# Last batch's down product joins x through the identity, fillers counted one by one, new leads

## The chip, the cores and the metric

The kernel runs on one core of one Trainium2 chip. The core's engines work in parallel, each in the order of its own instruction list: TensorE (PE in the profile; its weight loads are the row PEld), VectorE (DVE), ScalarE (ACT), GpSimd (POOL) and SyncE (SP), which issues the transfers between memory and on-chip storage. [...] The metric is the device time of one execution in microseconds, lower is better.

## The reference

There are 8 batches of 1024 rows with 128 features, all in f32. Cut to what matters, and with the weights that scale and shift left out:

```python
mod = (silu(c) @ wmod).reshape(8, 6, 1, 128)          # six vectors a batch: sa ca ga sb cb gb
h = layernorm(x) * (1 + ca) + sa
y = h
for i in range(6):                                    # six layers of linear attention and an MLP
    xn = layernorm(y)
    q, k, v = heads(xn @ wq[i]), heads(xn @ wk[i]), heads(xn @ wv[i])     # 8 heads of 16
    context = softmax(k, over rows).T @ v
    y = (softmax(q, over features) @ context) @ wo[i] + bo[i] + y
    y = leaky(layernorm(y) @ w1[i]) @ w2[i] + y       # 128 -> 512 -> 128
x = x + ga * y
h = layernorm(x) * (1 + cb) + sb
g = silu(fp4(h) @ fp4(w_gate).T) * (fp4(h) @ fp4(w_up).T)                 # 128 -> 352
x = x + gb * (fp4(g) @ fp4(w_down).T)                 # 352 -> 128
```

`fp4` takes each run of 16 values along the last axis, divides by its largest magnitude over 6, rounds to the FP4 grid and multiplies back. The last line is where the first part of the change sits: the down product is added to `x`.

## The kernel before

A batch is a tile of 128 partitions by 8 chunks of 128 features, worked in two halves of 512 columns. Four batches are in flight at a time, each in its own set of buffers (a lane), so batch 4 takes the place of batch 0 and so on. A batch has eight stages: the first norm and modulation (0), six layers (1 to 6) and the FP4 feed-forward part (7).

Nothing is run when the loops are walked. Every piece of work is added to a plan as a step with its engine, its planned duration, what it reads and what it writes (`add`), and `order` then writes the program out by hand. At each turn it takes, over all engines, the step that can start earliest; among equals it takes the one with the longest chain behind it plus a *lead*. `LEAD` holds one lead per batch and stage, and `TURNS` changes leads at planned times, given as a time and a list of batch, stage and lead. A change of ScalarE's function table is planned at 1.3. The order so found is fixed on each engine by explicit dependences, so a step whose operands are late holds back everything behind it on its engine.

Fillers are part of that order. When the step chosen for TensorE starts later than the engine is free, by more than `GAP` (0.35), `order` puts 128 by 128 products of the identity with itself into the gap, while a PSUM bank is free and until `BRINK` (0.1) before its end. In the first 11.5 planned us (`COLD`) a TensorE step counts double, and a filler too. Whether fillers count double is settled once per gap: one that begins before 11.5 has all its fillers at double length, and half the threshold. A filler appears as `warm<-ident` on line 1361.

The lines that the prediction speaks of, in the order of a batch. `layernorm` takes statistics on VectorE (L641, L647), `rstd` on ScalarE (L661 and L666, a logarithm and an exponential), the small steps L671 to L687 on VectorE, and applies it half on VectorE (L693) and half on ScalarE (L700). The result (`xh_a` ahead of the attention, `xh_m` ahead of the MLP, `h` ahead of the FP4 part) is transposed on TensorE (L719) and copied out by ScalarE with the norm's weights (`xT`, L929). A layer then has the key product (L949), its largest value `nmax` on VectorE (L956, joined at L963), the exponential `kT` on ScalarE (L972), the query product (L996) with `qmax` (L1005), the context (L1059 to L1100), the output product (L1126) added to `x` on VectorE (L1111), the MLP's w1 product (L1172), its leaky activation on ScalarE (L1181) and the w2 product (L1189). While the first layers run, `prepare_attn` folds the bias rows of all six layers (`mb_bc`, L611, and `wv_sb`, L618, after small products at L591 and L602).

In the FP4 part, `fp4` quantises `h` and later the gated product `g`: a maximum per run (L747), its scale (L754) and reciprocal (L759), the quotient `fv` (L763) on VectorE, the magnitude `fmag` (L773) on ScalarE, two rounding steps (L777, L784) on VectorE and the product with the scale (L792) on GpSimd, or on VectorE for the very last piece. Gate and up products are L1233, silu is L1241 on ScalarE, the product of the two L1249 on VectorE. Silu needs another function table than the norm's logarithm and the exponentials, so table loads stand ahead of the first silu and ahead of the first exponential after it (L1241, L1372).

`down` then takes a piece of `g`: three transposes per chunk (L1289), two copies `gT` on ScalarE (L1302), three products per chunk into one bank (L1313), and the sum onto `x` on VectorE (L1322). A batch has four pieces of two chunks; the last batch has six pieces, chunks 0–1, 2–3, 4, 5, 6 and 7. SyncE sends `x` out (L1265): halves, or for the last batch quarters, when their chunks are done. A product of f32 operands is two records in the trace.

Of the kernel before, what the change touches and what calls it, by code (L numbers as in the profile page):

```python
# [11 lines left out]
ALU = mybir.AluOpType  # L12
AX = mybir.AxisListType

P = 128
# [68 lines left out]
class Plan:  # L84
# [58 lines left out]
    def order(self, leads, turns, warm):  # L143
# [17 lines left out]
        while todo:  # L161
# [22 lines left out]
            cold = 2 if e == "PE" and free[e] < self.COLD else 1  # L184
            gap = e == "PE" and t - free[e] > self.GAP / cold
            while gap and min(bank_free) <= free[e]:
                to = free[e] + cold * mm(P)
                if to > t - self.BRINK:
                    break
                w, bank = Step(), bank_free.index(min(bank_free))  # L190
                w.fn, w.func = lambda bank=bank: warm(bank), None
                free[e] = bank_free[bank] = to
                out.append(w)
# [42 lines left out]
def mm(n):  # L236

    return 0.0115 + n * 1.654e-3
# [11 lines left out]
def kernel(  # L250
# [41 lines left out]
        [2405, 3996, 461, 247, -1202, -1296, -1300, -3196],  # L292
        [1413, 1593, 3441, 1928, -2207, 1189, 1781, -248],
        [366, -108, -1676, -2703, -3835, 1594, -2630, -2514],
        [-241, 558, -1413, 208, -413, 228, -5405, -156],
        [694, -3633, -2192, -2384, -870, -487, -1194, -1272],
        [-3687, 2479, 1403, 3083, -1193, -6, -811, -1034],
        [725, 1777, 204, -1637, -400, -327, -320, -670],
        [3404, 589, 1158, 1867, -7, -962, -419, -2719],
# [3 lines left out]
        (3, [(1, 0, -62)]),  # L303
        (27, [(3, 0, -535)]),
        (36, [(2, 1, -485)]),
        (39, [(3, 1, -531)]),
        (45, [(0, 2, 1516), (2, 1, -553)]),
        (48, [(2, 1, -544)]),
        (57, [(1, 1, 1518), (1, 2, 2846), (1, 3, 649)]),
        (75, [(1, 1, 1516)]),  # L310
        (90, [(1, 1, 773)]),
        (105, [(0, 3, 2919), (0, 4, 1470), (0, 5, 1376), (0, 7, -524)]),
        (120, [(0, 3, 2762), (2, 1, -721)]),
        (150, [(1, 2, -201)]),
        (165, [(2, 1, 797)]),
        (180, [(1, 2, 1215)]),
        (210, [(2, 2, 832)]),
        (225, [(3, 1, 914), (3, 6, -4315)]),
        (240, [(0, 5, 828)]),
        (255, [(0, 5, 2639), (0, 6, 2635)]),  # L320
        (270, [(2, 3, 156)]),
        (285, [(0, 7, 811), (1, 3, 64)]),
        (300, [(4, 0, -33)]),
        (315, [(2, 2, 1013), (4, 0, 939)]),
        (330, [(3, 2, 544)]),
        (345, [(0, 7, 348), (2, 3, -400)]),
        (360, [(0, 7, 811), (2, 3, 1746), (2, 4, -2375)]),
        (405, [(1, 4, -3784), (4, 1, -3690)]),
        (420, [(1, 4, -3786)]),
        (435, [(2, 4, -3941)]),  # L330
        (450, [(1, 4, -2313)]),
        (465, [(4, 1, -4514)]),
        (480, [(1, 5, 1477)]),
        (495, [(3, 5, 1525)]),
        (525, [(1, 5, 1515), (2, 5, 1254)]),
        (555, [(1, 7, 1337)]),
        (570, [(2, 5, 1311)]),
        (600, [(1, 7, 1342)]),
        (615, [(1, 7, 1337), (3, 6, -3519), (5, 2, 2464)]),
        (630, [(3, 7, 1425)]),  # L340
        (675, [(5, 1, 2181)]),
        (690, [(4, 1, -2521)]),
        (705, [(2, 7, -2804), (4, 2, -2786), (4, 3, -4487), (4, 7, -1958)]),
        (735, [(5, 2, 3162)]),
        (780, [(6, 1, 323)]),
        (795, [(2, 7, -2027)]),
        (810, [(3, 7, 2088), (5, 3, 1769)]),
        (825, [(4, 3, -2043)]),
        (840, [(5, 4, -2386), (7, 1, 210), (7, 2, 779)]),
        (870, [(4, 3, -2494)]),  # L350
        (885, [(7, 1, 493)]),
        (915, [(6, 2, 913)]),
        (930, [(4, 3, -1826), (4, 4, -1241)]),
        (945, [(5, 4, -2139), (5, 6, -1878)]),
        (975, [(6, 3, -2917)]),
        (1005, [(7, 4, -2167)]),
        (1020, [(5, 5, -1207)]),
        (1035, [(5, 5, -1166)]),
        (1065, [(7, 4, -1977)]),
        (1140, [(4, 6, -2161), (5, 6, -1912)]),  # L360
        (1155, [(4, 6, -1857)]),
        (1170, [(4, 7, -1928)]),
        (1245, [(5, 7, -1905)]),
        (1260, [(6, 7, -139)]),
        (1275, [(6, 6, -1635)]),
        (1305, [(5, 7, -1974), (7, 7, 205)]),
        (1320, [(6, 7, -143), (7, 6, -143)]),
        (1335, [(6, 7, 201)]),
        (1350, [(6, 7, 206), (7, 7, 207)]),
    ]  # L370
    LATE = 140.0
    NQ = 4
# [829 lines left out]
    def ffn(x, mod, b, ln):  # L1202
# [51 lines left out]
        for i, c0, cn in PIECES[b == B - 1]:  # L1254
            down(gs[c0 // G], c0 % G, cn, c0, wdb, x, f"{b}_{c0}", i % 2, DVE_LAST and b == B - 1 and c0 + cn == C)
# [15 lines left out]
    def down(g, g0, G, c0, wdb, x, name, i, last):  # L1271
# [36 lines left out]

        def dmm():
            for c in range(G):  # L1310
                for m, (k, kk) in enumerate(KS):
# [3 lines left out]
                        wdb.ap()[:kk, m, :], start=(m == 0), stop=(m == NK - 1),  # L1315
                    )

        add("PE", G * NK * mm(D), dmm, r=[gT, wdb], w=[td])

        def onto():  # L1320
# [100 lines left out]
```

## Time and profile before

| | before |
|---|---|
| median of 4 runs | 1400.73 us (1400.33 to 1401.67) |
| the profiled execution | 1401.4 us, of which 1399.7 are the span from first to last instruction |
| mean granted TensorE clock | 0.999 of full speed |
| busy: PE, DVE, ACT, POOL | 1387.3, 1136.0, 967.0, 250.1 us |
| fillers (L1361) | 142 records, 20.7 us |
| table loads on ScalarE | 21, mean 1283 ns |
| x added to the down product (L1322) | 30 of 128x256 and 4 of 128x128, from 350.1 to 1396.8 us |

In the profile a line names the engine, the line of the kernel, the operation, what it writes and reads (buffer numbers left out), the shapes and the number of instructions merged. Brackets at the end of a timeline line give the idle time ahead of it and what ended that. In the view by stretches each engine has its busy time and, in brackets, its instructions; then come the granted clock, the share of the transfer engines and their rate. Fillers count as busy, so a TensorE that is 99% busy is not 99% useful.

### The profile page before, as it was taken

How to read it: one execution, taken by the hardware profiler on the slowest of the kernel's cores; microseconds unless marked ns; L12 is line 12 of the kernel's file. 1: busy time of each engine (PE TensorE's matmuls, PEld its weight loads, DVE VectorE, ACT ScalarE, POOL GpSimd, SP SyncE). 2: the span in 40 equal slices, each digit the busy share in tenths (PEclk: the TensorE clock that was granted, in tenths of full speed). 3: DMA queues.
4: the chain of work that ended last, by engine and by line, in shares of the span. 5: the costliest groups of instructions: out<-in, count | busy, mean ns of one | idle time of the engine just before them, and what ended most of it. 6: DMA issues, size and time to landing. Idle time of an engine off the chain costs nothing. (4 is left out here: it accounts for less than half of the span.)

```text
span 1399.7 us, 26260 instructions
## 1 busy us (share of the span) xinstructions
PE 1387.3 (99%) x9149; PEld 1112.7 (79%) x9149; DVE 1136.0 (81%) x4504; ACT 967.0 (69%) x2284; POOL 250.1 (18%) x216
## 2 busy tenths in 40 slices
PE   8999999999999999999999999999999999999999
PEld 6779778877888887877787788787877887888877
DVE  8998747689878674999899999685767576899997
ACT  6786756676777765777768767676667667677674
POOL 2312000022201010223121241011011022122332
PEclk9999999999999999999999999999999999999999
DMA  7100000000000000000000000000000000000001
GB/s 219 48 1 1 1 1 1 1 17 12 16 1 1 1 1 1 16 12 18 31 12 13 0 31 1 1 1 1 1 1 1 1 1 1 2 1 1 16 8 38
DMA packets 16436, 18.77 MB, mean 13 GB/s; under 512 B 1600, under 2 KB 10536, under 8 KB 16304
## 3 DMA queue, kind: packets, MB, share of 16 engines
q1 hardware_dynamic: 16304, 17.10, 3.9%
q8 instruction: 72, 1.18, 0.4%
q14 instruction: 60, 0.49, 0.1%
HBM read 12.88 MB, written 4.22 MB: 12 GB/s over the span
## 5 line engine op out<-in xcount | busy, mean ns | idle before, releaser
L1172 PE MATMUL ps<-xT_m,w_sb 128*128 128x512 f32 x768 | 351.5, 593 | 1.3 <-ACT g L1241 0.9
L1172 PEld LDWEIGHTS ps<-xT_m,w_sb 128*128 128x128 f32 x768 | 136.3, 190 | 126.5 <-issue 90.9
L1037 POOL TENSOR_TENSOR q<-q,qsum 128x512 f32<-128x512 f32 x96 | 101.6, 1069 | 703.1 <-DVE qsum L1032 312.8
L1111 DVE TENSOR_TENSOR x<-ps,x 128x512 f32<-128x512 f32 x192 | 130.1, 681 | 112.0 <-PE ps L1189 96.7
L996 PEld LDWEIGHTS ps<-wq_sb,xT_a 128*128 128x128 f32 x768 | 96.5, 192 | 26.4 <-issue 16.3
L700 ACT ACTIVATE xh_a<-x,shift_a,rstd_a 128x128 f32<-128x128 f32 x192 | 83.3, 488 | 26.0 <-DVE shift_a L687 25.5
L1189 PEld LDWEIGHTS ps<-w_sb,hT_D 128*128 128x128 f32 x640 | 86.8, 192 | 15.8 <-issue 13.2
L996 PE MATMUL ps<-wq_sb,xT_a 128*128 128x128 f32 x768 | 98.7, 275 | 0.0
L949 PE MATMUL ps<-xT_a,wk_sb 128*128 128x512 f32 x192 | 97.2, 605 | 0.5 <-DVE stats_a L641 0.3
L1189 PE MATMUL ps<-w_sb,hT_E 128*128 128x128 f32 x640 | 97.6, 275 | 0.0
L1189 PE MATMUL ps<-w_sb,hT_C 128*128 128x128 f32 x640 | 97.6, 275 | 0.0
L1189 PE MATMUL ps<-w_sb,hT_B 128*128 128x128 f32 x640 | 97.6, 275 | 0.0
L1189 PE MATMUL ps<-w_sb,hT_D 128*128 128x128 f32 x640 | 97.5, 275 | 0.0
L1126 PEld LDWEIGHTS ps<-m,qT 128*128 128x128 f32 x768 | 91.4, 192 | 6.4 <-issue 1.4
L1059 PEld LDWEIGHTS ps<-k,xh_a 128*128 128x128 f32 x768 | 90.7, 192 | 6.4 <-issue 4.3
L1126 PE MATMUL ps<-m,qT 128*128 128x128 f32 x768 | 94.9, 275 | 0.0
L1059 PE MATMUL ps<-k,xh_a 128*128 128x128 f32 x768 | 93.4, 275 | 0.0
L700 ACT ACTIVATE xh_m<-x,shift_m,rstd_m 128x128 f32<-128x128 f32 x192 | 81.3, 486 | 17.3 <-DVE shift_m L687 17.1
L661 ACT ACTIVATE rstd_a<-mv_a,eps 128x4 f32<-128x4 f32 x96 | 28.4, 299 | 92.1 <-DVE mv_a L647 79.5
L641 DVE BATCH_NORM_STATS2 stats_a<-x 128x6 f32<-128x128 f32 x384 | 85.0, 277 | 1.6
L929 ACT ACTIVATE xT_m<-ps,cols 128x512 f32<-128x512 f32 x96 | 72.4, 776 | 20.0 <-PE ps L719 19.7
L1189 PEld LDWEIGHTS ps<-w_sb,hT_B 128*128 128x128 f32 x640 | 84.5, 192 | 0.7 <-issue 0.5
(181 smaller groups left out, 3210.7 us busy)
## 6 DMA issues: line engine op xcount, KB each, us to landing
x<-in_L_attn_x_dram SPq DMA_DIRECT2D x16, 256.0 KB, 3.0
out_dram<-x SPq DMA_DIRECT2D x14, 256.0 KB, 2.0
w_sb<-in_L_attn_w_dram SPq DMA_DIRECT2D x12, 256.0 KB, 4.3
mod<-mod_d SPq DMA_DIRECT2D x8, 256.0 KB
mod<-mod_d SPq DMA_DIRECT2D x4, 128.0 KB
out_dram<-x SPq DMA_DIRECT2D x4, 128.0 KB, 1.8
wk_sb<-in_L_attn_wk_dram SPq DMA_DIRECT2D x6, 64.0 KB, 3.4
wq_sb<-in_L_attn_wq_dram SPq DMA_DIRECT2D x6, 64.0 KB, 2.8
```

The source lines that it names most:

```text
L641: "DVE", 0.197, lambda c=c: nc.vector.bn_stats(stats.ap()[:, c, :], s(c)),
L661: lambda: nc.scalar.activation(y(), var(), AF.Ln, bias=eps),
L700: nc.scalar.activation(d(c), s(c), AF.Identity, bias=shift.ap()[:, c : c + 1], scale=rstd.ap()[:, c : c + 1],)
L929: lambda t=t, h=h: nc.scalar.activation(half(xT, h), t.ap(), AF.Identity, bias=col(params + 1, l), scale=col(params, l),),
L949: lambda tk=tk, h=h: nc.tensor.matmul(tk.ap(), wk_sb[:, l, :], half(xT, h), start=True, stop=True),
L996: nc.tensor.matmul(tq.ap()[:, c * D : (c + 1) * D], half(xT, h)[:, c * P : (c + 1) * P], wq_sb[:, l, :], start=True, stop=True,)
L1037: lambda h=h, hs=hs: nc.gpsimd.tensor_tensor(heads(half(q, h)), heads(half(q, h)), each(qsum.ap()[:, hs]), ALU.mult),
L1059: nc.tensor.matmul(tc_.ap()[:, :D], chunks(xh.ap())[:, c, :], chunks(k.ap())[:, c, :], start=(c == 0), stop=(c == C - 1),)
L1111: lambda: nc.vector.tensor_tensor(half(x, h), t.ap(), half(x, h), ALU.add),
L1126: nc.tensor.matmul(to.ap()[:, c * D : (c + 1) * D], half(qT, h)[:, c * P : (c + 1) * P], m.ap(), start=True, stop=True,)
L1172: lambda th=th, h=h, j=j: nc.tensor.matmul(th.ap(), w1_sb[:, l, j * P : (j + 1) * P], half(xmT, h), start=True, stop=True,),
L1189: nc.tensor.matmul(ty.ap()[:, c * D : (c + 1) * D], hidden(j)[:, c * P : (c + 1) * P], w2g.ap()[:, j, :] if l == L - 1 else w2_sb[:, l, j, :],
```

## The change

There are three parts.

1. **Fillers.** Whether a filler counts double is decided for each filler by the time at which it starts, and the threshold is `GAP` everywhere.
2. **The last batch's down product.** For batch 7 `down` opens each chunk's accumulation with a product of the identity and the chunk of `x`, so that the bank holds `x` plus the down product; ScalarE then copies the bank to `x`. The addition on VectorE is left out for this batch. The plan has the TensorE step read `x` and the copy write it; the transfer out follows the copy.
3. **Leads.** `LEAD` has new values and `TURNS` new times and values, 54 rows in place of 67. With them the order of nearly every engine's list changes after the first 41 us or so. On the engines the program has 90 fillers in place of 71, 8 products with the identity more, 29 table loads in place of 21, six copies more on ScalarE and six additions fewer on VectorE; the other instructions are the same in number.

Lines below the change move by 14 up to `down` and by one behind it: L1313 becomes L1307, L1361 becomes L1360, and the new copy is L1316, the new product L1301.

```diff
--- before.py
+++ after.py
@@ -181,10 +181,9 @@
                             best = (e, pick)
             assert best is not None
             e, (_, _, n, t, cost) = best
-            cold = 2 if e == "PE" and free[e] < self.COLD else 1
-            gap = e == "PE" and t - free[e] > self.GAP / cold
+            gap = e == "PE" and t - free[e] > self.GAP
             while gap and min(bank_free) <= free[e]:
-                to = free[e] + cold * mm(P)
+                to = free[e] + mm(P) * (2 if free[e] < self.COLD else 1)
                 if to > t - self.BRINK:
                     break
                 w, bank = Step(), bank_free.index(min(bank_free))
@@ -289,84 +288,71 @@
 
 
     LEAD = [
-        [2405, 3996, 461, 247, -1202, -1296, -1300, -3196],
...
-        [3404, 589, 1158, 1867, -7, -962, -419, -2719],
+        [2388, 3985, -262, 404, -1032, -1292, -1262, -3114],
...
+        [3382, 829, 1196, 2048, 15, -1506, -140, -2647],
     ]

     TURNS = [
-        (3, [(1, 0, -62)]),
-        (27, [(3, 0, -535)]),
-        (36, [(2, 1, -485)]),
...
-        (1335, [(6, 7, 201)]),
-        (1350, [(6, 7, 206), (7, 7, 207)]),
+        (3, [(2, 1, -130)]),
+        (33, [(1, 6, 216)]),
+        (36, [(2, 1, -267)]),
...
+        (1305, [(5, 7, -640)]),
+        (1320, [(7, 7, 476)]),
+        (1335, [(6, 7, 286), (7, 6, -662), (7, 7, 286)]),
     ]
     LATE = 140.0
     NQ = 4
@@ -1252,7 +1238,7 @@
 
         out = out_d[b].rearrange("(p c) d -> p c d", c=C)
         for i, c0, cn in PIECES[b == B - 1]:
-            down(gs[c0 // G], c0 % G, cn, c0, wdb, x, f"{b}_{c0}", i % 2, DVE_LAST and b == B - 1 and c0 + cn == C)
+            down(gs[c0 // G], c0 % G, cn, c0, wdb, x, f"{b}_{c0}", i % 2, DVE_LAST and b == B - 1 and c0 + cn == C, b == B - 1)
             done = c0 + cn
             if b == B - 1 and done % G == 0:
                 parts, n = [x[done // G - 1]], G
@@ -1268,7 +1254,7 @@
                 r=parts,
             )
 
-    def down(g, g0, G, c0, wdb, x, name, i, last):
+    def down(g, g0, G, c0, wdb, x, name, i, last, end):
 
 
         def src():
@@ -1306,22 +1292,35 @@
             )
         td = Ps(psum)
 
+        def xc():
+            return x.ap()[:, c0 * D : (c0 + G) * D]
+
         def dmm():
             for c in range(G):
+                if end:
+                    nc.tensor.matmul(
+                        td.ap()[:, c * D : (c + 1) * D], ident,
+                        xc()[:, c * D : (c + 1) * D], start=True, stop=False,
+                    )
                 for m, (k, kk) in enumerate(KS):
                     o = (m * G + c) * P
                     nc.tensor.matmul(
                         td.ap()[:, c * D : (c + 1) * D], gT.ap()[:kk, o : o + P],
-                        wdb.ap()[:kk, m, :], start=(m == 0), stop=(m == NK - 1),
+                        wdb.ap()[:kk, m, :], start=(m == 0 and not end), stop=(m == NK - 1),
                     )
 
+        xp = x[c0 // (C // NQ)]
+        if end:
+
+            add("PE", G * (NK + 1) * mm(D), dmm, r=[gT, wdb, xp], w=[td])
+            add("ACT", act(G * D), lambda: nc.scalar.copy(xc(), td.ap()[:, : G * D]), r=[td], w=[xp])
+            return
         add("PE", G * NK * mm(D), dmm, r=[gT, wdb], w=[td])
-
-        def onto():
-            xc = x.ap()[:, c0 * D : (c0 + G) * D]
-            nc.vector.tensor_tensor(xc, td.ap()[:, : G * D], xc, ALU.add)
-
-        add("DVE", vec(G * D), onto, r=[td], w=[x[c0 // (C // NQ)]])
+        add(
+            "DVE", vec(G * D),
+            lambda: nc.vector.tensor_tensor(xc(), td.ap()[:, : G * D], xc(), ALU.add),
+            r=[td], w=[xp],
+        )
 
 
     prepare_c()
```

## The prediction

> **What bounds the kernel now.** I read the page's engine shares first, then busy time by stretch, then the order of time at the two ends, then who waited for whom.
>
> ```profile
> span 1399.7 us, 26260 instructions
> PE 1387.3 (99%) x9149; PEld 1112.7 (79%) x9149; DVE 1136.0 (81%) x4504; ACT 967.0 (69%) x2284; POOL 250.1 (18%) x216
> ...
> core 0: us, PE busy (x) PEld busy (x) DVE busy (x) ACT busy (x) POOL busy (x), PEclk, DMA share, GB/s
> 20.00:22.00 2.00, 2.00 (x3) 0.91 (x4) 1.99 (x13) 2.00 (x6) 0.00 (x0) 0.50 0.74 232
> 22.00:24.00 2.00, 2.00 (x8) 1.02 (x7) 1.58 (x3) 1.89 (x7) 0.78 (x1) 0.64 0.79 219
> 300.00:600.00 300.00, 299.19 (x2006) 241.76 (x2005) 235.55 (x955) 203.67 (x482) 42.63 (x37) 1.00 0.02 8
> 600.00:900.00 300.00, 299.27 (x1958) 239.27 (x1957) 271.88 (x1023) 219.76 (x513) 70.86 (x55) 1.00 0.04 14
> 900.00:1200.00 300.00, 300.00 (x1997) 240.16 (x1997) 209.27 (x905) 199.15 (x471) 35.73 (x32) 1.00 0.00 1
> 1330.00:1362.00 32.00, 30.81 (x195) 24.00 (x194) 30.75 (x75) 23.27 (x48) 10.94 (x7) 1.00 0.03 9
> ...
> 10.27 4.51 PE L1361 MATMUL warm<-ident 128*128 128x128 f32 x38
> 15.86 0.30 PE L719 MATMUL ps<-ident,xh_a 128*128 128x128 f32 x1 [1.08 <-DVE xh_a L693]
> 19.86 3.66 PE L949 MATMUL ps<-xT_a,wk_sb 128*128 128x512 f32 x4 [0.16 <-ACT xT_a L929]
> 23.56 0.69 DVE L956 TENSOR_REDUCE nmax<-ps 128x1 f32<-128x512 f32 x1 [0.42 <-PE ps L949]
> 24.46 0.69 DVE L1005 TENSOR_REDUCE qmax<-ps 128x32 f32<-128x512 f32 x1 [0.22 <-PE ps L996]
> ...
> 1389.01 0.42 DVE L1322 TENSOR_TENSOR x<-ps,x 128x256 f32<-128x256 f32 x1
> 1389.63 0.29 DVE L1322 TENSOR_TENSOR x<-ps,x 128x128 f32<-128x128 f32 x1
> 1393.13 0.53 DVE L777 SCALAR_TENSOR_TENSOR fv_g<-fmag_g,fv_g 128x352 f32<-128x352 bf16 x1 [0.42 <-ACT fmag_g L773]
> 1396.81 0.29 DVE L1322 TENSOR_TENSOR x<-ps,x 128x128 f32<-128x128 f32 x1 [1.38 <-PE ps L1313]
> ...
> PE ps L1172 <- ACT g L1241: 0.9, 1, 0.9
> PE ps L1233 <- ACT g L1241: 0.3, 1, 0.3
> ```
>
> TensorE is the bound: from 50 to 1362 us the stretches (50 to 300 and 1200 to 1330 included, 249.94 and 130.00 busy) leave 2.8 us of idle. Only the ends have slack: at the head VectorE is full (20.00 of 20 us between 26 and 46) and fillers pad TensorE; at the tail, from 1368, one chain VectorE–ScalarE–GpSimd–TensorE quantises the last pieces. The rows at 20 to 24 us show the clock at half rate (3.66 us for four L949 records, later two take 1.02 to 1.10), and VectorE then waits 0.42 and 0.22. Whatever the middle of the new order does, its idle and its fillers go straight into the time.
>
> The profiled execution took 1401.4 us, 1.7 outside the span, and lies 0.7 above the median of 1400.73. The sum below is a difference; I put it on the median.
>
> **Part 1: fillers counted one by one.** The instruction lists have 90 fillers after, 71 before; 16 of the 19 come ahead of the first transposes of `xh_a`. A filler is two records; 12 took 1.50 us at 13.28, so (1.50 − 0.275)/11 = 0.111 each, 0.223 a filler. Before, fillers run from 10.27 to 14.78; with 35 they end at 10.27 + 35 × 0.223 = 18.1. The first transposes move from 15.86 to 18.1 and the eight end near 19.0. That costs nothing as long as ScalarE's `xT_a` copy is late anyway: it began at 19.04 behind the `cols` copy on VectorE (18.51 to 18.69), and the matmuls at 19.86 waited for it. Cover gone, it would cost up to 1. In return TensorE is busy through 16 to 20 us (2.77 of 4 before), and if the clock stays full the two VectorE waits go: −0.64. Next to be late is VectorE itself, so the other 1.2 us that the slow matmuls lose bring nothing.
>
> The Trainium skill ("TensorE: Matmul & The Clock Gate", Part 1) says that the clock falls after an idle window of 3.4 us, and that the window runs freely, so its phase differs between runs. The half rate here fits one such window: 0.50 from 20 to 22 and 0.64 over 22 to 24 put its end near 23.4. By the page the fix could matter in some runs only, and the term would lie between 0 and −0.64 by chance; the trace has one phase, and I go by it.
>
> **Part 2: new leads, head.** The order is the same up to about 41 us. There, between batch 0's `mv_m` (done 39.66) and its `xh_m`, VectorE did for batch 2 two `nmax` reduces (0.67 each) and their join (0.07), and two `mb_bc` steps (0.2 each); after, these stand behind `xh_m`, and four BN statistics of 0.2 stand ahead. Net 1.8 − 0.8 = 1.0 earlier. On ScalarE the `kT` exponential of batch 2 (0.69 from 42.55) also goes behind: `xh_m` began at 43.23, its shift was ready at 42.85, so 0.38 more. With the 0.64 the first w1 matmul (45.93) comes 2.0 us earlier. But 0.66 us of TensorE's work (batch 2's `kT` transposes above all) is then still to do, so the gain is 2.0 − 0.66 = 1.35. Ends: 0 (batch 2, pushed back, starves TensorE before 60 us) and −2.3.
>
> **Part 3: new leads, middle.** Batches 6 and 7 start later in the new order, and the last batch's six layers follow one another with fewer others between. Four fillers appear where before had none from 50 to 1360: one ahead of a w1 group of batch 7's first layer, three around `xh_m` of its third. TensorE runs in order, so they cost 4 × 0.223 = 0.9, and I add 0.3 for what is left of the gaps around them: +1.2. Lower end: all 2.8 us of visible idle vanishes and the fillers stay, −1.9. Upper end: each of batch 7's six layers loses the longest wait in the trace's middle (0.92), +5.5. I take the value close to the order's own marks because the trace shows nearly no idle for a reshuffle to win back, and 900 to 1330 shows none at all.
>
> ScalarE gets 8 more table loads (29 against 21), four more changes between exp and silu, and its in-order queue stands still behind each (evictions and norms of the other lanes). A load takes 1283 ns: 10.3 us on an engine 69% busy. What TensorE felt of ten silu changes is the two waits for `g`, 0.92 and 0.34, so 0.13 a change: 4 × 0.13 = +0.5. Ends: 0 and 4 × 0.92 = +3.7.
>
> The Trainium skill ("ScalarE: Activation LUTs", What ACT_TABLE_LOAD costs) puts a drain of 1380 ns beside the load, about 2.66 us a switch, which speaks against this change. The trace differs: a load began at 1331.23, lasted 1.28, and the silu began at 1332.52. By the page ScalarE would lose 21 us, and the term, by an estimate from the page, might double to +1.
>
> **Part 4: the tail up to the last batch's gates.** TensorE has done the same work when the first half of `h_7` is transposed. Around there the new order has 8 fillers where before had 5: 3 × 0.223 = 0.7. An extra pair of table loads stands between the two halves of `h_7`, and the second half's `rstd` now queues behind a magnitude step (0.79) of batch 6. Part of that hides behind gate matmuls (1367 to 1372): +0.8 in all; ends 0 and +2.
>
> **Part 5: x through the identity.** Eight matmuls (16 records, 8 × 0.223 = 1.8 us) fall where TensorE ran 30 fillers or waited; only the second one of each of the two 2-chunk pieces stands behind the wait for `gT`, 0.22 each. VectorE loses six adds. Three lie ahead of its last quantising steps: 1383.72 (0.42, by its own row) and the two shown, 0.42 + 0.29, together 1.13. The one at 1392.42 saves nothing, since L777 then waits 0.42 for `fmag` anyway; the one at 1395.14 is behind the last `g`; the last becomes a ScalarE copy, 266 ns (the `gxk` copies) for 289. The brake: ScalarE is in order, and the copy of piece 4 stands ahead of `fmag` of piece 6, that of piece 2 ahead of `gT` of piece 4. Piece 4's sum is ready about 1389.6 and copied by 1389.9, where `fmag` of piece 6 could start at 1389.7; what is late next is this copy. I take −0.8; ends −1.15 (no brake) and +0.5 (a 368 ns copy in front of `gT` on top, VectorE's relief unused). SP issues the same transfers, now behind ScalarE; POOL's list is unchanged in number.
>
> **Sum.** −1.35 + 1.2 + 0.5 + 0.8 − 0.8 = +0.35, so 1401.1 us.
>
> **Rivals.**
> 1. *Slower: the late last batch starves TensorE.* Place: 1000 to 1200 us and batch 7's layers. For it: the new fillers in the middle, the later start of batches 6 and 7. Against: no idle there before with the same four lanes. Price: five or six waits of 0.92 in place of the 1.2, +4.3 on the sum, 1405.4. It decides from 1403.5, that is from about 3.6 us of idle and fillers there.
> 2. *Faster: the new order removes the stalls as well.* Visible idle (2.8) gone with the four fillers unneeded in effect: middle −1.9 in place of +1.2, tables 0, head −1.35, tail 0: −3.3, 1397.4. For it: 1.2 of the 2.8 is at 1331 to 1333, behind one table load. Against: more such loads.
> 3. *Fillers do not do what they are for*: the clock still halves and the late transposes hold `xT_a`: head 0 in place of −1.35, or +1; 1402.5 to 1403.5.
> 4. *The copies brake ScalarE*: part 5 is +0.5, 1402.4.
>
> **How the numbers follow.** A measurement can tell about 0.2%, 2.8 us, from no change: 1397.9 to 1403.5. The forecast with rivals 3 and 4 has 0.45, all within; rival 1 has 0.30; rival 2 0.25. The forecast's own range is 1398.5 to 1403.5. Adding the ends gives −1.35 − 1.9 − 1.15 = −4.4 (tables and tail 0; 1396.3) and +4.3 + 3.7 − 1.35 − 0.8 + 0.8 = +6.7 with rival 1's middle taken as +4.3 (1407.4). Leaving about 1 in 10 out on each side: 1396.5 to 1406.5. Faster 0.25, same 0.45, slower 0.30.
>
> **What would show it.** Head: PEclk 1.00 from 20 to 24, four L949 records in about 2 us, the first w1 matmul near 43.9. Middle: TensorE's idle from 50 to 1362 plus the mid fillers at most 4 us. Tables: 29 loads, silu waits (`g`) below 2 us. Tail: from the first gate matmul of `h_7` to the end 0 to 1 us shorter. I am wrong if idle in the middle passes 4.5 us, if it falls below 1, or if the first matmul of batch 0's MLP does not move.

## The result, and the profile after

The changed kernel takes 1402.97 us in the median of 34 runs (1401.82 to 1403.47). The kernel before, run beside it again, takes 1401.34 in the median of 52 (1400.07 to 1402.92). The ratio is 1.0011 with a 95% interval of 1.0006 to 1.0016: 1.6 us slower, within the 0.2% that the forecast called no change, but a loss by its interval. The prediction was 1401.1 with a range of 1396.5 to 1406.5, and "same" as the likeliest. PSUM below is the memory that TensorE writes its products to (`ps` in the rows); SBUF holds the other tiles.

The changed kernel's page and its view by stretches, with the columns of the lines shown of before (TensorE, its weight loads, VectorE, ScalarE, GpSimd, each with instructions; granted clock; DMA share; GB/s):

```profile
span 1401.5 us, 26425 instructions
PE 1390.0 (99%) x9203; PEld 1118.0 (80%) x9203; DVE 1136.9 (81%) x4498; ACT 985.1 (70%) x2298; POOL 249.9 (18%) x216
...
20.00:22.00 2.00, 1.84 (x5) 0.86 (x5) 2.00 (x15) 2.00 (x6) 0.00 (x0) 1.00 0.65 131
22.00:24.00 2.00, 2.00 (x19) 1.96 (x17) 2.00 (x5) 2.00 (x7) 0.51 (x1) 1.00 1.00 302
50.00:100.00 50.00, 49.11 (x347) 40.70 (x346) 48.70 (x216) 40.06 (x102) 12.55 (x11) 1.00 0.01 1
300.00:600.00 300.00, 299.79 (x1978) 240.89 (x1978) 258.89 (x1006) 217.58 (x509) 59.63 (x49) 1.00 0.04 11
600.00:900.00 300.00, 299.39 (x1997) 241.31 (x1996) 223.36 (x934) 200.14 (x472) 38.43 (x34) 1.00 0.02 6
900.00:1200.00 300.00, 298.68 (x1995) 240.39 (x1994) 240.28 (x958) 214.91 (x496) 57.78 (x47) 1.00 0.02 6
1330.00:1362.00 32.00, 31.80 (x202) 24.89 (x201) 30.61 (x76) 23.53 (x45) 10.03 (x7) 1.00 0.03 10
```

The clock now stays at 1.00 from 20 to 24 us. The middle's idle has moved: 0.9 us between 50 and 100 and 1.3 between 900 and 1200, where before had none; 300 to 600 lost 0.6 of its idle and 1330 to 1362 a whole 1.0. The order of time on TensorE, and who it waited for between 50 and 1330 us:

```profile
9.79 7.99 PE L1360 MATMUL warm<-ident 128*128 128x128 f32 x67
17.61 1.04 PE L705 MATMUL ps<-ident,xh_a 128*128 128x128 f32 x8
20.22 1.98 PE L935 MATMUL ps<-xT_a,wk_sb 128*128 128x512 f32 x4 [0.16 <-ACT xT_a L915]
44.57 5.74 PE L1158 MATMUL ps<-xT_m,w_sb 128*128 128x512 f32 x13
67.06 1.32 PE L705 MATMUL ps<-ident,kT 128*128 128x128 f32 x8 [0.88 <-ACT kT L958]
...
PE ps L705 <- ACT kT L958: 1.3, 2, 0.9
PE ps L705 <- DVE xh_m L679: 0.8, 2, 0.5
PE ps L1079 <- DVE ctxT L1071: 0.6, 1, 0.6
```

The four key products take 1.98 us (3.66 before). The first w1 product comes at 44.57 (45.93), and at 67 a new wait of 0.88 stands: the exponential `kT` of batch 1's first layer is late on ScalarE. No wait for silu (`g`) is left in the middle.

To see where time goes, five moments were read from the order of time of every trace: the first w1 product, the last w2 product of the program, the first transposes of `h_7`, the first transposes of the last batch's `g`, and the end of the span. TensorE does the same real work up to each of them in every kernel here, except that the new order has put off 0.87 us of it (transposes of `kT`, and small products) past the first w1 product, and that the identity products fall in the last stretch.

| kernel | first w1 product at | to the last w2 product | to `h_7` | to `g_7` | to the end |
|---|---|---|---|---|---|
| before | 45.93 | 1308.03 | 12.22 | 14.62 | 18.87 |
| changed | 44.57 | 1310.22 | 13.36 | 14.96 | 18.39 |
| filler counting alone | 45.53 | 1308.17 | 12.22 | 14.63 | 18.88 |
| new leads alone | 45.94 | 1310.26 | 13.36 | 14.97 | 18.61 |
| the sum alone, order of before | 45.09 | 1307.96 | 12.22 | 14.62 | 18.85 |
| filler counting and sum, order of before | 44.42 | 1308.01 | 12.22 | 14.62 | 18.84 |

Apart from the head, a stretch repeats to 0.2 us or better when its order is the same. From the first w1 product on, the changed kernel is 3.19 slower (1356.93 against 1353.74).

The head differs between executions of one order, first by when x arrives, so it is counted here from the start of ScalarE's first `xT_a` copy (19.04 before, 19.41 in the changed kernel) to the first w1 product. All traces of this study give:

| order, clock between 20 and 22 us | length of the head | mean |
|---|---|---|
| before, half | 26.89, 26.10, 26.66 | 26.55 |
| before, full | 25.67, 26.03, 25.14, 25.58, 25.71 | 25.63 |
| new leads, half | 26.57 | |
| new leads, full | 25.16, 25.17, 25.11, 25.18 | 25.16 |

The heads of before at full clock scatter by 0.9, and the only half-clock head of the new leads is no shorter than those of before; the account of the prediction's part 2 therefore also measures it from where the order changes.

### The profile page after: what moved, and what is told of

Its sections match the earlier page's. It is cut to its first block, busy times and chain, and to the rows that moved or that the text cites. A ratio compares the mean times of both kernels' runs of the same rounds, so it can differ in the third digit from the quotient of the medians.

```text
span 1401.5 us, 26425 instructions
## 1 busy us (share of the span) xinstructions
PE 1390.0 (99%) x9203; PEld 1118.0 (80%) x9203; DVE 1136.9 (81%) x4498; ACT 985.1 (70%) x2298; POOL 249.9 (18%) x216
## 4 chain that ended last, share of the span: by engine, by line
PE 87%; DVE 10%; ACT 2%; issue 1%; DMA 0%; POOL 0%; SPq 0%; DVEq 0%; ACTq 0%
PE ps L1158 23%; PE ps L1175 22%; PE ps L705 11%; PE ps L1045 5%; PE ps L1112 5%; PE ps L982 5%; PE ps L935 5%; PE ps L1219 5%; PE ps L1307 2%; PE ps L1275 1%; DVE x L1097 1%; DVE stats_a L627 1%; PE ps L1079 1%; PE ps L1054 1%; DVE xh_m L679 1%; DVE stats_m L627 1%
## 5 line engine op out<-in xcount | busy, mean ns | idle before, releaser
L915 ACT ACTIVATE xT_a<-ps,cols 128x512 f32<-128x512 f32 x96 | 72.7, 779 | 20.5 <-PE ps L705 20.2
L958 ACT ACTIVATE kT<-ps,nmax 128x512 f32<-128x512 f32 x96 | 65.2, 684 | 28.6 <-DVE nmax L949 28.4
```

Source lines behind the costliest of these rows:

```text
L915: lambda t=t, h=h: nc.scalar.activation(half(xT, h), t.ap(), AF.Identity, bias=col(params + 1, l), scale=col(params, l),),
```

## The experiments

Medians are of about 11 runs, 6 to 11 where noted, each beside the kernel before on the same chip. The first four take the change apart. Their medians of before are 1401.43, in the second four 1401.29, in the third three 1401.72, in the last 1401.31.

### Filler counting alone

```diff
-            cold = 2 if e == "PE" and free[e] < self.COLD else 1
-            gap = e == "PE" and t - free[e] > self.GAP / cold
+            gap = e == "PE" and t - free[e] > self.GAP
...
-                to = free[e] + cold * mm(P)
+                to = free[e] + mm(P) * (2 if free[e] < self.COLD else 1)
```

> Only the counting of the fillers is changed; 16 more fillers stand ahead of the first transposes of the head, and the rest of every engine's order is that of before. Theory A (the head is bound by VectorE, the half-rate clock costs its two waits): the clock is 1.00 from 20 to 24 us, the waits 0.42 and 0.22 go, the time falls by 0.6 to 0.7. Theory B (the phase of the clock's window differs from run to run, which is why runs of the kernel before lie 2.9 us apart and those of the changed kernel mostly within 0.6): the runs come to lie within about 1 us of one another, near the lowest of before (1400.1), so 1.0 to 1.3 below the median of before. Rival (fillers delay the first transposes): 0 to +0.5.

Measured 1400.20 (1398.96 to 1401.14), ratio 0.9994 (0.9985 to 1.0002), so this run alone does not set the gain clear of nothing; with the sum added (below) the interval does. The fall of 1.2 is nearer to theory B's size, and the runs lie 2.2 apart where those of before lie 4.2 apart, though not within 1.

The record has the mean granted clock of every execution, and it settles where the gain comes from. Of 99 executions of the kernel before, 21 have 1.000 and a median of 1400.25, 44 have 0.999 and 1401.34, and 34 have less and 1402.13. All 108 executions of the kernels with the new counting have 1.000. At full clock the kernel before is as fast as this one, so what the fillers take away is the half-rate stretches. It also means that the changed kernel, always at full clock, is 2.7 slower than before at full clock.

The stretches after the first w1 product are those of before, so the gain is the head's; with the new counting it is 25.61 long in the mean of four traces, with the half-rate clock 26.55: 0.94.

### New leads alone

```diff
     LEAD = [
-        [2405, 3996, 461, 247, -1202, -1296, -1300, -3196],
+        [2388, 3985, -262, 404, -1032, -1292, -1262, -3114],
...
     TURNS = [
-        (3, [(1, 0, -62)]),
+        (3, [(2, 1, -130)]),
...
```

> Only LEAD and TURNS are new; fillers are counted and x is added as before. Theory (the new order costs 1.4 in the middle and 1.4 ahead of the last batch's feed-forward part, and gives back 0.4 in the head): 2.0 to 3.0 slower than before, with stalls near 66, 940 to 990 and 1157 us as in the changed kernel. Rival (the loss of 1.6 sits in the identity products and copies or in the fillers): within 0.5 of before.

Measured 1404.63 (1401.84 to 1405.36, 10 runs), ratio 1.0022 (1.0013 to 1.0031): 3.2 slower, a little over the upper end. The stretches of the table are the changed kernel's, but for the last. So the whole loss, and more, sits in the leads.

### The sum alone, with the order of before

The sum is emitted as in the change, but the plan still places a VectorE addition, so every other instruction keeps its place.

```diff
+                if end:
+                    nc.tensor.matmul(
+                        td.ap()[:, c * D : (c + 1) * D], ident,
+                        x.ap()[:, (c0 + c) * D : (c0 + c + 1) * D], start=True, stop=False,
+                    )
...
+            if end:
+                nc.scalar.copy(xc, td.ap()[:, : G * D])
+                return
```

> Only the last batch's sum is changed: identity products open the accumulation and ScalarE copies, each copy where the planned addition stood, and the order of all else, fillers and leads are those of before. Theory (VectorE is relieved of up to 1.13, the copies ahead of a magnitude step take half of it back, as the changed kernel's trace has it): 0.4 to 0.6 faster. Without a brake: 1.1 faster. Rival (the copies hold ScalarE back by as much as they relieve VectorE): 0 to +0.5.

Measured 1401.14 (1399.83 to 1402.53), ratio 0.9997 (0.9988 to 1.0006): no difference, the rival's end. The last stretch is 18.85 (18.87 before). VectorE was relieved and gained nothing. Its quotient steps (L763) and GpSimd's products (L792) in the order of time, first before, where the addition stands between:

```profile
1383.72 0.42 DVE L1322 TENSOR_TENSOR x<-ps,x 128x256 f32<-128x256 f32 x1
1384.07 0.79 DVE L763 TENSOR_TENSOR fv_g<-g,rec_g 128x352 f32<-128x352 f32 x1
1389.84 0.51 DVE L763 TENSOR_TENSOR fv_g<-g,rec_g 128x352 f32<-128x352 f32 x1
...
1383.08 1.39 POOL L792 TENSOR_TENSOR g<-fv_g,scale_g 128x704 f32<-128x704 f32 x1 [2.65 <-DVE fv_g L784]
1389.10 0.78 POOL L792 TENSOR_TENSOR g<-fv_g,scale_g 128x352 f32<-128x352 f32 x1 [1.45 <-DVE scale_g L754]
```

and without the addition:

```profile
1382.84 1.10 DVE L763 TENSOR_TENSOR fv_g<-g,rec_g 128x352 f32<-128x352 f32 x1
1388.55 0.80 DVE L763 TENSOR_TENSOR fv_g<-g,rec_g 128x352 f32<-128x352 f32 x1
...
1382.17 1.39 POOL L792 TENSOR_TENSOR g<-fv_g,scale_g 128x704 f32<-128x704 f32 x1 [2.65 <-DVE scale_g L754]
1388.18 0.78 POOL L792 TENSOR_TENSOR g<-fv_g,scale_g 128x352 f32<-128x352 f32 x1 [1.45 <-DVE scale_g L754]
```

GpSimd's product starts 2.28 after the first transposes of `g_7` in both (1382.17 − 1379.89, and 1383.08 − 1380.81 = 2.27) and lasts 1.39. The quotient starts 0.31 earlier without the addition, takes 1.10 in place of 0.79, and ends at the same moment. Where it starts only as GpSimd's product ends (1389.84, product to 1389.88), it takes 0.51. In the second pair it starts 0.37 earlier without the two additions ahead of it, takes 0.80, and ends 0.08 earlier. So an addition that reads PSUM ran beside GpSimd at no cost, and the quotient, which reads two operands from SBUF, waits for GpSimd to finish.

The Trainium skill ("GPSIMD Engine Reference", section 1) says the two engines contend over SBUF when a VectorE instruction has two SBUF inputs. The rows above (0.51 unhindered, 0.79 to 1.10 beside a product) agree.

### Filler counting and the sum together, order of before

Both edits above.

> The filler counting and the last batch's sum together, on the order and the leads of before. If the two parts add up: 1.1 to 1.9 faster than before, and so 2.5 to 3.5 faster than the changed kernel; that would leave the whole loss to the leads. Rival (the gain of the head is lost on the way, in a stall of the middle): 0.4 to 0.6 faster, as the sum alone.

Measured 1400.43 (1398.69 to 1400.89), ratio 0.9990 (0.9981 to 0.9998), 2.5 below the changed kernel. The two parts do not add up: the sum added nothing to the filler counting. All parts but the leads are worth the 1.0 to 1.2 of the fillers.

### The changed kernel without the fillers of the middle

```diff
-            gap = e == "PE" and t - free[e] > self.GAP
+            gap = e == "PE" and t - free[e] > self.GAP and not 48.0 < free[e] < 1300.0
```

> The changed kernel without its four fillers of the middle (planned times 48 to 1300); the order of all else is the same. If TensorE, in order, pays them in full (the prediction's reading): 0.9 to 1.1 faster than the changed kernel, seen as a stretch from the first w1 matmul to the last w2 matmul shorter by that. If they only fill time in which the next operand is late anyway: no change of that stretch (within 0.2).

Measured 1402.89 (1402.25 to 1403.16): the changed kernel's time. The stretch to the last w2 product is 1310.01, 0.21 less. Two of the places, changed kernel first, then without:

```profile
1156.13 0.61 PE L1360 MATMUL warm<-ident 128*128 128x128 f32 x4
1156.58 0.71 PE L705 MATMUL ps<-ident,xh_m 128*128 128x128 f32 x5
1157.82 0.55 PE L705 MATMUL ps<-ident,xh_m 128*128 128x128 f32 x3 [0.54 <-DVE xh_m L679]
1158.21 0.39 PE L1360 MATMUL warm<-ident 128*128 128x128 f32 x2
1158.43 1.02 PE L1158 MATMUL ps<-xT_m,w_sb 128*128 128x512 f32 x2
```

```profile
1156.23 0.93 PE L705 MATMUL ps<-ident,xh_m 128*128 128x128 f32 x5
1157.91 0.55 PE L705 MATMUL ps<-ident,xh_m 128*128 128x128 f32 x3 [0.75 <-DVE xh_m L679]
1158.29 1.02 PE L1158 MATMUL ps<-xT_m,w_sb 128*128 128x512 f32 x2
```

The three fillers go and the wait for `xh_m` ends where it did. These fillers cost next to nothing by themselves (0.2 for four); they mark places where the last batch's operand is late.

### The changed kernel with the addition of before

```diff
-                if end:
+                if False:
...
-            add("ACT", act(G * D), lambda: nc.scalar.copy(xc(), td.ap()[:, : G * D]), r=[td], w=[xp])
+            add("ACT", act(G * D), lambda: nc.vector.tensor_tensor(xc(), td.ap()[:, : G * D], xc(), ALU.add), r=[td], w=[xp])
```

> The changed kernel with the last batch's sum as before: no identity products, VectorE adds, each addition where the planned copy stood; fillers, leads and the order of all else as in the changed kernel. From the two tails (18.39 us from the first transposes of the last batch's g to the end, 18.61 with the new leads alone): 0.2 slower than the changed kernel. By the prediction's own term: 0.8 slower. If the copies brake as much as they relieve: no difference.

Measured 1403.64 (1403.19 to 1404.03), 0.7 slower than the changed kernel; the last stretch is 19.11 against 18.39. Here the additions stand where copies were planned, and the three ahead of the last quantising steps are not beside GpSimd's products, so the sum through the identity is worth its 0.7. With the additions planned as additions (new leads alone) the stretch is 18.61. The edit's worth runs from 0.0 to 0.7, depending on where the additions would otherwise lie.

### The changed kernel with two table loads less near the end

Batch 6's last two silus are moved ahead of the root of `h_7`'s first norm half.

```diff
+    silu = [s for s in acts if s.stage == (B - 2, 1 + L) and s.func == "silu"][-2:]
+    root = next(s for s in acts if s.stage == (B - 1, 1 + L) and s.func == "exp")
+    seq = [s for s in seq if s not in silu]
+    at_root = seq.index(root)
+    seq[at_root:at_root] = silu
```

> The changed kernel with the two silu steps of batch 6's last gates moved ahead of the root of the last batch's first norm half on ScalarE, which takes away two table loads (one silu, one exp) around 1350 to 1361; nothing else moves. If these two loads make the last batch's h late: the stretch from the last w2 matmul to the first transposes of h (13.36, against 12.22 before) gets 0.8 to 1.2 shorter and the end comes as much earlier. If VectorE's queue is what makes it late (the second half's x is added 2.1 later than before): under 0.3.

Measured 1404.70 (1404.38 to 1404.89, 8 runs): 1.7 slower than the changed kernel, and the stretch to `h_7` is 14.93, 1.57 longer. Neither expectation had this. From the order of time of this kernel:

```profile
1348.87 0.99 ACT L1227 ACTIVATE g<-ps 128x352 f32<-128x352 f32 x2 [1.37 <-PE ps L1219]
1349.87 1.28 ACT L1378 ACT_TABLE_LOAD   x1
1351.16 0.30 ACT L647 ACTIVATE rstd_f<-mv_f,eps 128x4 f32<-128x4 f32 x1
...
1351.73 0.16 DVE L657 SCALAR_TENSOR_TENSOR shift_f<-mv_f,rstd_f 128x4 f32<-128x4 f32 x1 [1.52 <-ACT rstd_f L652]
```

The moved silus wait 1.37 for TensorE's gate products, and behind them the root starts at 1351.16 (1349.10 in the changed kernel), so VectorE, which is never idle there otherwise, waits 1.52. The move thus brings a wait of its own and does not isolate the loads. That the loads are not what makes `h_7` late follows from the changed kernel's trace: from 1347.2 to 1366.6, where VectorE ends the rounding of `h_7`'s first half, it is busy 19.14 of 19.40 us, so it waited for neither load nor root.

### The kernel before with six more table loads

```diff
+        if table == "exp" and getattr(step, "eng", None) == "ACT" and acts in AGAIN:
+            nc.scalar.preload_act_table_set("natural_log_exp_and_others")
```

> The kernel before with six more table loads on ScalarE, one each at six places of the middle between 180 and 700 us, the set being the one already loaded; nothing else moves. By the prediction's price of 0.13 a pair: 0.2 to 0.8 slower, the stretch from the first w1 to the last w2 matmul (1308.0) longer by that. If each costs TensorE the longest wait seen behind one (0.92): 4 to 5.5 slower. If ScalarE's slack hides them: 0 to 0.2.

Measured 1401.83 (1401.17 to 1403.01), ratio 1.0004 (0.9995 to 1.0013). The stretch to the last w2 product is 1308.57, 0.54 longer: 0.09 a load. The prediction's price of 0.13 a pair was about right; the eight loads of the change would cost some 0.7 at this price.

### The kernel before with more VectorE work before the end

```diff
+        def peak():
+            for _ in range(MORE if n == "g6_6" else 1):
+                nc.vector.tensor_reduce(
```

> The kernel before with one reduction on VectorE (the largest value per run of batch 6's last piece of g, 0.8 a time, about 1352 us) done four times in place of once: 2.4 us more VectorE work shortly before the last batch's h is quantised; the result is the same and nothing moves. If the end phase is bound by VectorE's remaining work (the changed kernel has about 2.7 more of it, like for like, after its last w2 matmul): 1.5 to 2.4 slower, most of it in the stretch from the last w2 matmul to the first transposes of the last g. If ScalarE's table loads or TensorE's own order set that stretch: under 0.8.

Measured 1405.25 (1405.18 to 1406.60, 6 runs), ratio 1.0030 (1.0018 to 1.0041). The four reductions take 3.64 where one took 0.87, 2.8 more, and the stretch to `h_7` grows by 4.16 (16.38); the others stay. It is over the range; between the medians the loss is 3.5. VectorE and TensorE of this kernel, then ScalarE of before at the same place:

```profile
1352.64 3.64 DVE L748 TENSOR_REDUCE scale_g<-g 128x44 f32<-128x704 f32 x4
...
1360.90 4.57 PE L1314 MATMUL ps<-wdb,gT 128*128 128x128 f32 x24 [2.33 <-ACT gT L1303]
```

```profile
1356.73 0.30 ACT L661 ACTIVATE rstd_f<-mv_f,eps 128x4 f32<-128x4 f32 x1 [3.10 <-DVE mv_f L647]
1357.39 1.61 ACT L1302 COPY gT<-ps 128x512 f32<-128x512 f32 x4
```

In before, ScalarE already waits 3.10 for VectorE's statistics of `h_7`'s second half, with batch 5's `gT` copies queued behind. What VectorE is late passes through ScalarE's order to TensorE, which waits 2.33. The rest is the clock: behind that wait it is granted at half rate from 1361.2 to 1364.6, though the copies are done at 1361.87, and the products take 4.57 in place of 2.91:

```profile
1361.20:1364.60 3.40, 3.40 (x18) 3.40 (x17) 3.38 (x12) 2.83 (x7) 0.00 (x0) 0.50 0.16 58
```

So VectorE's 2.8 cost about 2.5 by themselves and 1.7 by the clock. In the changed kernel the clock is 1.00 to the end, and only the first applies.

### Early silu loads on the kernel before

With the new filler counting, each silu load is issued right behind the last exponential-table function ahead of it.

```diff
+    before_silu = {id(s) for s, t in zip(funcs, funcs[1:]) if s.func == "exp" and t.func == "silu"}
...
+        if id(step) in before_silu:
+            nc.scalar.preload_act_table_set("silu_and_others")
```

> The kernel before with the new filler counting, and every silu table load issued right behind the last exponential-table function ahead of it in place of right ahead of the first silu; nothing else moves. Theory (the stalls of before near 331, 618 and 1331 us stand behind a load that holds up the first silu, 0.5 to 1.5 each): the middle's stalls fall by 1 to 2, and with the fillers 1399 to 1400 results, below both kernels. Rival (the load only moves its 1.28 to another step of a full ScalarE): within 0.4 of the filler counting alone (1400.2).

Measured 1402.64 (1402.07 to 1402.90), ratio 1.0007 (0.9998 to 1.0016): 2.4 slower than the filler counting alone (2.2 when each is taken against its own median of before), against both expectations. The wait at 1331 is gone, but the last load now stands behind the root of `h_7`'s second half and ahead of the `gT` copies, and TensorE waits for them:

```profile
1357.23 1.28 ACT L1378 ACT_TABLE_LOAD   x1
1358.52 1.61 ACT L1301 COPY gT<-ps 128x512 f32<-128x512 f32 x4
...
1359.16 2.94 PE L1312 MATMUL ps<-wdb,gT 128*128 128x128 f32 x24 [1.44 <-ACT gT L1301]
```

The stretch to `h_7` is 13.86 (12.22). The price of a load is one of place: 1.6 here, 0.1 on average in the middle.

### No fillers in the head

```diff
-            gap = e == "PE" and t - free[e] > self.GAP / cold
+            gap = e == "PE" and t - free[e] > self.GAP / cold and not 6.0 < free[e] < 20.0
```

> The kernel before without the fillers of planned times 6 to 20 in the head; the order of all else is the same. If fillers hold the clock up, and half rate costs what the two traces of the head say: the clock at half rate around 18 to 24 us in every run, the first w1 matmul 0.6 to 1 later than with the new counting, 0.6 to 1.3 slower than that (1400.8 to 1401.5), so near the kernel before, which is at half rate in some runs. If the clock's phase alone decides and fillers do nothing: the same spread as before.

Left out are 42 of the head's 78 filler records, those of planned times 6 to 20. Measured 1402.14 (1401.42 to 1402.74), 1.9 slower than with the new counting (1.7 when each is taken against its own median of before). Granted clock in the stretches 16 to 20, 20 to 22 and 22 to 24 us of this kernel:

```profile
16.00:20.00 4.00, 2.78 (x11) 1.80 (x11) 4.00 (x38) 3.25 (x11) 0.00 (x0) 0.50 0.79 219
20.00:22.00 2.00, 2.00 (x3) 0.84 (x3) 1.86 (x12) 2.00 (x6) 0.00 (x0) 0.50 0.76 247
22.00:24.00 2.00, 2.00 (x6) 1.10 (x5) 1.58 (x3) 1.70 (x6) 0.85 (x1) 0.50 0.88 236
```

Half rate throughout, and VectorE has gaps (1.86 and 1.58 of 2) that the other head lacks. From the first `xT_a` copy to the first w1 product it is 27.67, 2.06 more than the mean with the new counting.

### One early load

As above, for batch 6's load alone.

```diff
+    before_silu = {id(s) for s, t in zip(funcs, funcs[1:]) if s.func == "exp" and t.func == "silu" and t.stage[0] == 6}
```

> The filler counting alone, and of the silu loads only batch 6's, the one near 1331 us, issued earlier: behind the last norm root of batch 7's sixth layer, where ScalarE waits for VectorE. The load behind the root of the last batch's second half, which in the run with all loads early kept the gT copies back and cost 1.6, stays where it was. If TensorE's stall of 1.1 at 1331 is worth its length at the end: 0.6 to 1.0 faster than the filler counting alone (1400.2), the stretch from the first w1 to the last w2 matmul 1307.2 to 1307.6 in place of 1308.2. If the end phase waits for VectorE, which does no less: that stretch shorter, the next one (12.22) longer by as much, and the time 1400.0 to 1400.4.

Measured 1399.87 (1399.24 to 1400.54), ratio 0.9990 (0.9981 to 0.9999): the lowest median here, 3.1 below the changed kernel. Against the filler counting alone it is 0.3 lower (0.2 when each is taken against its own median of before), less than the runs can tell. In the trace the first stretch is 1307.23, 0.94 shorter, and the next 12.43, 0.21 longer, so 0.73 is kept. That VectorE's end phase takes back the 0.21 is likely, not shown.

## Why the prediction was right or wrong

**The direction and the range held; the sum was +0.35 and the measured change +1.6.** That it came so near is in part luck: the terms missed by up to 1.1 in both directions. Its parts, by the moments of the table:

| term | predicted | shown |
|---|---|---|
| fillers and clock (part 1) | −0.64 | −0.9 in the heads' means, −1.2 in the medians |
| leads, head (rest of part 2) | −0.71 | +0.4 (+0.2 from where the order changes) |
| middle, with tables (part 3) | +1.7 | +1.3 |
| up to the last gates (part 4) | +0.8 | +1.5 |
| the sum (part 5) | −0.8 | −0.5, of it −0.3 by the order |

The shown terms add up to −0.9 + 0.4 + 1.3 + 1.5 − 0.5 = +1.8; the medians have 1.6.

Of the signs that it named, the head's clock and key products, the 29 loads, the silu waits and the tail (0.13 shorter from the first gate product of `h_7`) came. The first w1 product stands at 44.57 and not near 43.9, and the middle has 3.25 of idle and 1.4 of fillers (2.45 with those after 1330), more than the 4 that it allowed. None of its three signs of being wrong came. The upper end of its range has a slip: rival 1's +4.3 is what it adds to the 1.2, so the ends add up to 1408.6 and not 1407.4; nothing came near either.

**Part 1** had the mechanism right: more fillers, full clock, VectorE's two waits gone. The size was low. One trace of before cannot give it: with the old counting four of five traces have 0.50 between 20 and 22 us and one has 1.00, with the new counting all eight have 1.00, with none it is half rate for longer. The cover named there held: with the transposes later, the `xT_a` copy still starts 3.68 after the first `xh_a` step (15.73 to 19.41, and 15.37 to 19.04 before). Its sentence that by the page the fix could matter in some runs only is what the clocks of the executions show: 78 of 99 of before lost some clock.

**Part 2** failed in its step "so the gain is 2.0 − 0.66 = 1.35". The order changes only behind the last `mv_m` of batch 0. From there to the first w1 product the nine traces of the old order take 5.85 to 6.46 (mean 6.14) and the five of the new one 5.36 to 5.48 (mean 5.42), whatever the clock: 0.7 sooner, not the 1.38 (1.0 and 0.38) of the prediction. The work put off is 0.87 and not 0.66. So the head loses 0.2 for TensorE, or 0.4 by the means of whole heads. Part of the miss is in the rows: five statistics, not four, stand ahead of `xh_m`, and the shift was ready at 42.93, not 42.85, which leaves 0.8 and 0.3. The rest stays open. One thing that neither order avoids stands in the order of time at 40 us, before and changed:

```profile
41.07 1.29 POOL L1141 TENSOR_TENSOR w2g<-w_sb,mod 128x512 f32<-128x512 f32 x1 [8.12 <-DMA mod<-mod_d]
41.38 1.07 DVE L676 SCALAR_TENSOR_TENSOR shift_m<-shift_m,rstd_m 128x4 f32<-128x4 f32 x2
42.93 1.10 DVE L693 TENSOR_SCALAR xh_m<-x,mv_m,rstd_m 128x128 f32<-128x128 f32 x4
```

```profile
40.73 1.56 DVE L679 TENSOR_SCALAR xh_m<-x,mv_m,rstd_m 128x128 f32<-128x128 f32 x2
40.75 1.45 POOL L1127 TENSOR_TENSOR w2g<-w_sb,mod 128x512 f32<-128x512 f32 x1 [8.38 <-DMA mod<-mod_d]
42.28 0.59 DVE L679 TENSOR_SCALAR xh_m<-x,mv_m,rstd_m 128x128 f32<-128x128 f32 x2
```

GpSimd's product `w2g` holds VectorE up wherever it falls: a `shift_m` pair in one (1.07 where 0.22 is usual), the first `xh_m` in the other (1.56 for two, then 0.59). Both orders pay for it (0.85 and 0.97 more than usual), so it does not explain the miss. The lower end that was written beside it, a starved TensorE because a batch was pushed back, came at 67 us, with batch 1's `kT` in place of batch 2's.

**Part 3** had nearly the right sum from wrong terms. "TensorE runs in order, so they cost 4 × 0.223" is refuted: without the fillers 0.2 is gained. What the middle costs is in the waits. Taking each record's start against the steady step of its group, and counting fillers as idle, the new order has, against before, about +1.4 between 50 and 100 us, −3.5 between 100 and 900, +4 between 900 and 1300, and −1.0 at 1331. Rival 1 (a late last batch starves TensorE) and rival 2 (the new order removes the stalls) both happened in part, one after the other, and nearly cancelled; that the sum came out is luck. The forecast's "nearly no idle for a reshuffle to win back" was wrong: the visible idle of 2.8 was less than what the starts show (about 6.4).

The tables' price of 0.13 a pair was borne out as a size by the added loads (0.18 a pair), but in the changed kernel no wait for silu is left at all. The drain that the Trainium skill (“ScalarE: Activation LUTs”, What ACT_TABLE_LOAD costs) puts beside a load was not seen: the silu or the copy follows the load's end by about 0.01.

**Part 4** named the wrong cause. Its extra fillers and its pair of loads are there, but `h_7` itself is late, by way of VectorE. After the last w2 product VectorE ends the last rounding of `h_7`'s first half at 11.85 (9.30 before), GpSimd's product delivers it at 13.06 (10.83) and TensorE transposes at 13.36 (12.22). TensorE's extra time there is 14 filler records in place of 10 (0.44) and a wait of 0.58 for VectorE's additions. Nearly half of VectorE's 2.55 is one small step, in the changed kernel:

```profile
1363.24 1.34 DVE L662 SCALAR_TENSOR_TENSOR shift_f<-shift_f,rstd_f 128x4 f32<-128x4 f32 x1
1362.82 1.75 POOL L778 TENSOR_TENSOR g<-fv_g,scale_g 128x704 f32<-128x704 f32 x1 [4.02 <-DVE shift_f L657]
1366.79 1.06 POOL L778 TENSOR_TENSOR h<-fv_x,scale_x 128x512 f32<-128x512 f32 x1 [2.22 <-DVE fv_x L770]
1368.15 0.60 PE L705 MATMUL ps<-ident,h 128*128 128x128 f32 x4
```

The step takes 1.34 where 0.15 is usual, while GpSimd's product runs from 1362.82 to 1364.57. The rest is order: VectorE has more left to do. It is busy for 38.64 us after the last w2 product in the changed kernel and 37.93 before, although six additions are gone; like for like (both with additions, or both with the sum) it is 1.4 to 2.2 more. That VectorE work added just there delays `h_7` by about its length is shown by a run. That the step beside GpSimd and the extra work are what moved `h_7` by 1.1 is read from the traces; no run took either away, nor the fillers there.

**Part 5** priced VectorE's instructions by their length. The 1.13 of additions ahead of the last quantising steps did not stand on VectorE's chain alone: at 1383.72 and again at 1389 the quotient behind them had to wait for GpSimd anyway. The brake that was priced (copies ahead of `fmag` and `gT`) exists, but the term that failed is the relief. In the old order the term is 0.0, between the −0.8 and rival 4's +0.5, and not for rival 4's reason; in the new one the additions cost 0.2 to 0.7, near the −0.8 where they were not planned.

Rival 3 (the fillers fail) fell with the filler run.

## What to carry to other kernels

On an engine that is full and in order, a new instruction order should be judged by the sum of its stalls over the whole span, and by each engine's work left at the start of the end phase; local marks such as fillers or a table load show where something is late, not what it costs. Take a compound change apart at once: here a gain of 1.2 from a few fillers lay hidden under a new order that cost about 3. Compare executions at the same granted clock: the median of before mixes them. Before an instruction is moved off a busy engine, look whether it ran beside another engine that the next instruction must wait for.

## What the runs showed of the hardware

- **The half-rate clock comes and goes between executions of one program.** With the old number of fillers the clock between 20 and 22 us was 0.50, 0.50, 0.50, 0.50 and 1.00 in five traces whose heads have the same fillers, and 78 of 99 executions had a mean clock below 1.000. The half-rate stretches of the head last 3.41 us (before, 20.01 to 23.43), 6.83 (new leads alone) and 10.24 (without the head's fillers), which is one, two and three times the shortest; in before TensorE's longest gap ahead of it, from 10 us on, was 1.08. More fillers made it 1.00 in all of eight traces and 1.000 in all of 108 executions.
- **GpSimd's products hold up some of VectorE's steps and not others.** In the trace of before, the norm's `xh` step of 128x128 takes 0.34 alone and 1.08 to 1.31 in all ten cases that start while a GpSimd product runs; small steps on two SBUF operands of 128x4 take 0.15 alone and up to 1.38. The quotient takes 0.51 unhindered, 0.79 beside a product there and 1.10 without the addition ahead of it. The norm's statistics (0.28) and additions that read PSUM (0.68 for 128x512) take the same either way.
- **A table load's cost is its place**: 0.09 each over six places of the middle, 1.6 ahead of the `gT` copies that TensorE waits for.
- **A wait of TensorE near the end cost clock as well**: 2.33 us of idle behind 2.8 us of added VectorE work, then 3.4 us at half rate, 4.2 in all up to `h_7` and 3.5 between the medians.
